# Holding only GpSimd's additions at a change of batch, in a kernel of four-way scans over an image

## The chip, the core and the metric

The kernel runs on one core of a Trainium2 chip. The metric is the device time of one execution in microseconds (us); of several executions the median is taken. A profile is one execution recorded by the hardware profiler; its times are counted from the start of its span.

## What is computed

The input `x` holds 4 images (the batch) of 128 channels and 96 by 96 pixels. Each image is normalised over groups of channels and laid out as four sequences of 9216 pixels: row by row (H), that reversed, column by column (V), and that reversed. Each sequence goes through the same block, the results are put back at their pixels, projected and added to `x`. Cut to what matters here:

```python
t = grouped1x1(x, in_proj_w, in_proj_b)            # 128 -> 512 channels
u, gate = t[:, :HID], t[:, HID:]
u = depthwise_conv(silu(u), dw_w)                  # 5 taps along the sequence
s = conv1x1(u, ssm_in_w); a = decay(conv1x1(u, ssm_delta_w))
bb = tanh(conv1x1(u, ssm_b_w)); cc = tanh(conv1x1(u, ssm_c_w))
prefix = cumsum(log(a))
hst = exp(prefix) * cumsum(bb * s * exp(-prefix))  # a linear recurrence
u = u + conv1x1(cc * hst + d * s, ssm_out_w)
y = conv1x1(grouped1x1(u * sigmoid(gate), mix_w), out_proj_w)
out = x + fuse_w @ concat(y of the four sequences) # with fuse_b
```

## The kernel before, in words

**Units and pairs.** Work is cut into units of 384 positions of one sequence. A unit has a batch, an order (V or H), a stage `st` of six, one of four interleaved phases `p`, and a direction `s` (0 forward, 1 reversed). The two directions of the same `st` and `p` make a pair; there are 384 units and 192 pairs, 48 to a batch: first 24 in V order, then 24 in H order. `pair(t)` issues everything of turn `t`. The order on every engine is written out by hand in the program (a manual schedule), and each engine takes its own instructions in that order.

**What one turn holds.** For pair `t` itself it computes the convolution of the first half of the channels on TensorE (`conv`, `conv_less`), the taps of the second half on VectorE (`taps`, L651), and the projections `proj`, 32 matmuls shown as `psum<-u,main`, with their Tanh and copies on ScalarE (L683, L684, L689) and the decay and drive on GpSimd (L691, L692). For pair `t+4` it computes the input projection and Silu (`front`, L495) where the sequence is fresh; the second half of each order reads the mirrored results of the first half back from DRAM. For the pair six turns back, `bi = 2*(t-6)`, it computes or rereads the gates (`gates_and_out`, Tanh at L537), multiplies by the state's output matrix (`out_of`, L520) and gates on VectorE (`gating`, L599 and L600). `recurrence` issues the scan on VectorE (L718) and the output steps on GpSimd (`outputs`, L724, L725 and the copy L727).

**The output products.** The gated units of turn `t` go to the list `waiting`. In the next turn `accumulate` multiplies each by the fused output matrix (16 matmuls, shown as `psum<-u,w_fin`), copies the result from PSUM to an SBUF tile `ys` on ScalarE (L751 with the bias, L753 without) and returns `add`, which adds `ys` to the accumulator `acc` on GpSimd (L770). `ys` has the pool's two buffers. `acc` is one tile for the whole image; it starts as the batch's `x` and ends as its output. A turn has two places for products: the first ahead of the gates (L845, bank `w[0]`) and the second either at L853, or behind the gating (L880, bank `w[1]`). Ahead of both come the turn's convolution matmuls.

**PSUM.** [...] The projections use banks 4 and 5 (`PROJ`). In a turn with a front, `plan` gives the convolution banks 4 and 5 and the products banks 7 and 6; in a turn without one, the convolution gets banks 7 and 6 and the products banks 4 and 5. The gates of a turn with a front go to banks 6, 4, 5 and 7.

**The change of batch.** When a batch's last additions are done, `send` issues four stores of `acc` on the DMA queue of SyncE (L733), and in the next turn four loads bring the next batch's `x` into the same places (L819), each behind its store. The first two units of the new batch come to their products in that turn. It is called `late`: `bi` is 98, 194 or 290, that is `t` = 55, 103 and 151. In a late turn the kernel before leaves the first place empty. It puts the first product in the second place and keeps its `add`; after the projections it issues that `add`, the whole second product (bank 6 again) and the second addition (L893 to L895):

```python
if waiting and not late:
    accumulate(waiting.pop(0), w[0], *final)()
...
if waiting:
    add = accumulate(waiting.pop(0), w[1])
    if not late:
        add()
...
proj(i, PROJ if back else banks, between)
...
if late:
    add()
    accumulate(waiting.pop(0), w[1])()
```

Turn 55 has a front, turn 56 has none. At the change from V to H inside a batch (turns 31 and 32 of the first) the same kinds of turn follow each other, and nothing is late there.

Of the kernel before, what the change touches and what calls it, by code (L numbers as in the profile page):

```python
# [42 lines left out]
F32 = mybir.dt.float32  # L43
# [4 lines left out]
P = 128  # L48
# [11 lines left out]
N = LN * WW // R  # L60
# [7 lines left out]
def conv_preact_kernel(  # L68
# [9 lines left out]
    nc = tc.nc  # L78
# [46 lines left out]
    def plan(with_front):  # L125

        return (PROJ, FRONT[:2]) if with_front else (FRONT[:2], PROJ)

    def bank(i):
        return psum[:, i, :]  # L130

    def mm(o, col, lhsT, rhs, start, stop):
        r = slice(32 * col, 32 * col + 32)
        nc.tensor.matmul(o[r, : rhs.shape[-1]], lhsT, rhs, start=start, stop=stop,  # L134
                         skip_group_check=True)
# [110 lines left out]
    def fresh(step):  # L246

        return step * UB < NU and step % NS < NS // 2
# [11 lines left out]
    def mirror(n):  # L260

        return None if n % NP < NP // 2 else NP - 1 - n % NP
# [124 lines left out]
    wk = ctx.enter_context(tc.tile_pool(name="work", bufs=2))  # L387
# [40 lines left out]
    def front(i, banks):  # L428
        for _ in front_parts(i, banks):
            pass  # L430
# [94 lines left out]
    def under(bi, s):  # L525

        seeded.add(bi)
        nc.scalar.copy(psum[:, SSM + 2 * s : SSM + 2 * s + 2, :N], us[bi][:, s])  # L528
# [21 lines left out]
    def load_kept(n):  # L550
        m = mirror(n)
        if n < NU // 2 - R and m is not None and m < NP // 2 - 2:
            old_gates[n] = gates[m % 2]
            nc.sync.dma_start(old_gates[n], kept[n // NP % 2][m])
# [58 lines left out]
    def conv(i, banks):  # L613

        step, p = units[i]["step"], units[i]["p"]
        sil, k, b0 = blocks(step), less_of(p), min(banks)
        for s in range(2):
            for g in range(4):
                mm(bank(b0 + s), g, band[:, s, p, g, :], columns(step, sil[s][:, g, :], 1 - k),
                   True, False)  # L620
# [15 lines left out]
    def new_u(i):  # L636
        us[i] = wk.tile([P, 2, 2, N], F32, tag="u", bufs=LAG + 2, name=f"u_{units[i]['id']}")
# [65 lines left out]
    def first_tap(i):  # L703
        if i < NU:
            taps(i, range(1))
# [25 lines left out]
    def send():  # L731
        for b, r in done:
            nc.sync.dma_start(out[b, :, r], accf[:, r])  # L733
            if b + 1 < B:
                reload.append((b + 1, r))
        done.clear()

    def accumulate(bu, bk, adder=nc.gpsimd, last=False):

        b, s, p, st = bu["b"], bu["s"], bu["p"], bu["st"]  # L740
        py = bank(bk)
        direct = last and (s == 1 or bu["order"] == "H")
        for j in range(2):
            for c in range(4):
                mm(py, c, w_fin[:, bu["dir"], j, 32 * c : 32 * c + 32], bu["v"][:, j, :],
                   j == 0, j == 1)
        y = py[:, :N]
        if not direct:
            ys = wk.tile([P, N], F32, tag="ys", name=f"ys_{bu['id']}")
            if s == 0 and bu["order"] == "H":  # L750
                nc.scalar.activation(ys, y, AF.Identity, bias=b_fin)  # L751
            else:
                nc.scalar.copy(ys, y)  # L753
            y = ys
        if s == 1:
            y, p, st = y[:, ::-1], R - 1 - p, NS - 1 - st
        if bu["order"] == "V":
            part = acc.rearrange("p (m q) r c -> p m q r c", q=R)[
                :, :, p, :, bass.ds(st * LN // R, LN // R)
            ]  # L760
            y = y.rearrange("p (c r m) -> p m r c", r=R, m=M)
        else:
            part = acc[:, bass.ts(st, LN), p, :]
            y = y.rearrange("p (h m) -> p h m", m=M)

        def add():
            if direct and s == 0:
                adder.scalar_tensor_tensor(part, y, b_fin, part, ALU.add, ALU.add)
            else:
                adder.tensor_add(part, y, part)  # L770
            if bu["order"] == "H" and bu["st"] >= NS // 2 and bu["p"] == R - 1:

                done.extend((b, bass.ts(2 * st + e, LN * WW // 2)) for e in range(2))

        return add
# [1 line left out]

    later, soon = [], []

    waiting = []  # L780

    def recurrence(t):
        i, k = 2 * t, t % R
        if k < 2 and 0 <= t // R - 1 < NU // UB:
            scan(t // R - 1, k)
        if 0 <= i - 10 < NU:
            outputs(i - 10)

    def head_banks(t):

        return PROJ if t % 2 or t >= LAG else FRONT[1::-1]

    def pair(t):
        i, k, bi = 2 * t, t % R, 2 * (t - LAG)
        back = bi >= 0
        old = back and mirror(bi // 2) is not None

        late = bi > 2 and (bi - 2) % (NU // B) == 0
        with_front = fresh((t + R) // R)
        final = (nc.vector, True) if t == NU // 2 - 1 else ()  # L800
        seed = old or back and not with_front

        ahead = old or back and not with_front
        banks, w = plan(with_front or not back)
        if not back:
            banks = head_banks(t)
        if back:
            front(t + R, FRONT)
        for n in soon:
            load_kept(n)  # L810
        soon.clear()
        if seed and not with_front:
            under(bi, 1)
        if t < NU // 2 - 2:
            send()

        if len(reload) == 4 and (k == 1 or late):
            for b, r in reload:
                nc.sync.dma_start(accf[:, r], xr[b, :, r])  # L819
            reload.clear()  # L820
        if t:
            new_u(i)
            taps(i, range(1, K))
            conv(i, banks)
        if t and not ahead:
            conv_less(i, banks)
        if not back:
            first_tap(i + 2)
            if t:
                front(t + R, FRONT if banks == PROJ else (5, 4, 2, 3))  # L830
        recurrence(t)
        un = units[i]
        stats_chunks(t)

        def stats_piece():
            if later and k > 1:
                next(later[0], None)

        if not ahead:
            free[0] = w[1]  # L840
            stats_piece()
        if seed and with_front:
            for s in (1, 0):
                under(bi, s)
        if waiting and not late:  # L845
            accumulate(waiting.pop(0), w[0], *final)()

        between = ahead and not old
        if between:
            conv_less(i, banks)  # L850
        if seed and not with_front:
            under(bi, 0)
        if ahead:  # L853
            accumulate(waiting.pop(0), w[1], *final)()
            free[0] = w[0]
            if not between:
                conv_less(i, banks)
            stats_piece()
        if old:
            scale_s(i - 2)  # L860
            for s in range(2):
                for j in range(2):
                    out_of(bi, s, j)
                load_gate(bi + s + UB)
        elif back:
            gates_and_out(bi, with_front)
        if back:
            for s in range(2):
                gating(bi, s)
        if un["order"] == "V" and un["b"] + 1 < B and un["st"] == NS - 1 and k == R - 1:  # L870
            later[:] = [stats_finish(un["b"] + 1)]
        if t + 1 < NU // 2:
            load_chunks(t + 1)
        if back:

            if k == 2 and t + 1 < NU // 2:
                soon.append(bi // 2 + 2)
            else:
                load_kept(bi // 2 + 2)
            if waiting:  # L880
                add = accumulate(waiting.pop(0), w[1])
                if not late:
                    add()
            first_tap(i + 2)
        if t == NU // 2 - 1:
            for s in range(2):
                under(bi + 2, s)
        if t == NU // 2 - 1:
            outputs(i - 8, None)
        proj(i, PROJ if back else banks, between)  # L890
        if not old and t > 0:
            scale_s(i - 2)
        if late:  # L893
            add()
            accumulate(waiting.pop(0), w[1])()  # L895
        if back:
            waiting.extend(units[bi : bi + 2])
        if t >= NU // 2 - 4:
            load_last(t)

        keep_silu((1, 2, 1, 0)[t] if t < R else 0)

        if bi > 0 and bi % (NU // B) == 0:
            send()
# [217 lines left out]
```

## Time and profile before

| what | value |
|---|---|
| median of 3 runs | 1839.7 us (1839.36 to 1840.79) |
| profiled execution, whole | 1833.3 us |
| its span, first to last instruction | 1831.6 us |
| TensorE, busy | 1806.8 us (99%) |
| ScalarE, busy | 1566.0 us (86%) |
| VectorE, busy | 1448.8 us (79%) |
| GpSimd, busy | 1423.5 us (78%) |
| granted TensorE clock, mean | 0.996 |

The lines of the profile that follow are read thus. PE is TensorE's matmuls, PEld its weight loads, DVE VectorE, ACT ScalarE, POOL GpSimd, SP SyncE; `L134` is line 134 of the kernel, and since all small matmuls go through one helper, their tiles tell them apart. In a table of waits, `PE psum L134 <- ACT ys L753: 3.1, 3, 1.1` says that TensorE stood still ahead of a matmul of L134 until ScalarE's L753 was done: 3.1 us in all, 3 times, 1.1 us at the longest. In a timeline a line has the start, the length, the engine, the line, the operation, output and inputs, and in brackets the idle time ahead of it. Matmuls overlap, and their ends are modelled.

### The profile page before, as it was taken

Reading aid. Unit: us, or ns where it says so; the run is one execution under the profiler, and the core shown is the slowest. Engines: PE = TensorE matmul, PEld = TensorE weight load, DVE = VectorE, ACT = ScalarE, POOL = GpSimd, SP = SyncE. Lnnn points to the kernel's source line nnn. Section 1 sums busy time; section 2 is a strip of 40 time slices with the busy share of each in tenths; the row PEclk is TensorE's granted clock in tenths of the full one; section 3 lists DMA queues with packets and bytes.
Section 4 is the critical chain, followed back from the end, with each engine's and each line's share of the span. In section 5 each row is a group of like instructions: output and inputs, shape, how many; then the busy total and the mean of one; then the engine's idle time right before and its main releaser. Section 6 shows DMA issues by size and latency. Waiting matters only on the chain.

```text
span 1831.6 us, 57282 instructions
## 1 busy us (share of the span) xinstructions
PE 1806.8 (99%) x24068; PEld 653.9 (36%) x24068; DVE 1448.8 (79%) x1451; ACT 1566.0 (86%) x2762; POOL 1423.5 (78%) x1469
## 2 busy tenths in 40 slices
PE   7999999999999999999999999999999999999998
PEld 4333333333333333333333333333333333333333
DVE  5888878877878888877778888877877778777886
ACT  4888888988888888888898888888888888888975
POOL 2487887778777888787877888787877788887785
PEclk8999999999999999999999999999999999999999
DMA  6755563444965566244696546443476634535434
GB/s 196 200 191 179 164 192 108 161 144 147 307 227 181 167 188 190 102 142 140 214 296 207 165 162 211 136 152 110 162 236 223 234 123 152 192 109 179 148 122 156
DMA packets 147825, 321.18 MB, mean 175 GB/s; under 512 B 14192, under 2 KB 115696, under 8 KB 147568
## 3 DMA queue, kind: packets, MB, share of 16 engines
q1 hardware_dynamic: 147136, 316.56, 53.1%
q8 instruction: 190, 3.11, 0.7%
q10 hardware_dynamic: 432, 0.96, 0.1%
q14 instruction: 67, 0.55, 0.1%
HBM read 185.21 MB, written 132.25 MB: 173 GB/s over the span
## 4 chain that ended last, share of the span: by engine, by line
PE 96%; ACT 2%; DMA 1%; DVE 1%; issue 0%; SPq 0%; POOL 0%; ACTq 0%; DVEq 0%; POOLq 0%
PE psum L134 82%; PE psum L520 8%; PE psum L514 5%; ACT sil L495 0%; DMA x_in<-in_xs 0%; DMA fuse<-in_fuse 0%; PE psum L286 0%; DVE u L600 0%; ACT t L701 0%; ACT t L689 0%; PE psum L364 0%; ACT psum L649 0%; DMA out<-acc 0%; ACT u L632 0%; DVE psum L651 0%
## 5 line engine op out<-in xcount | busy, mean ns | idle before, releaser
L651 DVE SCALAR_TENSOR_TENSOR psum<-sil,small,psum 128x768 f32<-128x768 f32 x576 | 588.9, 1022 | 33.2 <-ACT psum L649 7.4
L600 DVE SCALAR_TENSOR_TENSOR u<-gate,psum 128x768 f32<-128x768 f32 x376 | 349.6, 952 | 256.6 <-ACT gate L537 118.6
L134 PE MATMUL psum<-u,w_fin 128*32 128x384 f32 x6176 | 551.7, 487 | 0.2 <-ACT t L689 0.2
L134 PE MATMUL psum<-u,main 128*32 128x384 f32 x6144 | 536.4, 490 | 0.1
L770 POOL TENSOR_TENSOR acc<-ys,acc 128x384 f32<-128x384 f32 x374 | 412.2, 1122 | 33.3 <-ACT ys L751 9.1
L724 POOL TENSOR_TENSOR t<-t,t 64x384 f32<-64x384 f32 x191 | 234.9, 1230 | 158.4 <-PE psum L514 78.8
L134 PEld LDWEIGHTS psum<-u,w_fin 128*32 128x32 f32 x6176 | 189.1, 110 | 320.8 <-issue 218.7
L134 PEld LDWEIGHTS psum<-u,main 128*32 128x32 f32 x6144 | 181.6, 110 | 327.6 <-issue 199.1
L528 ACT COPY psum<-u 128x768 f32<-128x768 f32 x352 | 276.9, 800 | 20.7 <-DVE u L651 10.2
L691 POOL TENSOR_SCALAR t<-tm 64x384 f32<-64x384 f32 x191 | 177.0, 927 | 151.0 <-ACT tm L683 100.8
L134 PE MATMUL psum<-sil,band 128*32 128x384 f32 x3072 | 286.8, 489 | 3.1 <-ACT ys L753 3.1
L725 POOL TENSOR_TENSOR t<-t,t 64x384 f32<-64x384 f32 x191 | 246.4, 1290 | 15.0
L520 PE MATMUL psum<-t,main 32*128 32x384 f32 x1536 | 241.9, 513 | 3.3 <-ACT psum L528 2.6
L649 ACT ACTIVATE psum<-sil,small 128x768 f32<-128x768 f32 x192 | 174.1, 907 | 63.2 <-DVE u L600 53.7
L537 ACT ACTIVATE gate<-psum,bnorm 128x384 f32<-128x384 f32 x384 | 192.6, 582 | 28.9 <-PE psum L514 26.9
L692 POOL TENSOR_TENSOR t<-t,tm 64x384 f32<-64x384 f32 x192 | 195.0, 1016 | 15.4 <-ACT t L684 0.2
L651 DVE SCALAR_TENSOR_TENSOR u<-sil,small,psum 128x768 f32<-128x768 f32 x192 | 194.9, 1015 | 7.8
L495 ACT ACTIVATE sil<-psum,bnorm 128x385 f32<-128x385 f32 x384 | 191.7, 584 | 3.6 <-PE psum L134 1.4
L134 PE MATMUL psum<-sil,less 64*32 64x384 f32 x3072 | 168.2, 495 | 0.0
L514 PE MATMUL psum<-x_in,wn 32*128 32x384 f32 x768 | 162.0, 528 | 2.3 <-ACT u L632 1.2
L753 ACT COPY ys<-psum 128x384 f32<-128x384 f32 x281 | 129.9, 476 | 30.2 <-PE psum L134 29.2
L134 PEld LDWEIGHTS psum<-sil,band 128*32 128x32 f32 x3072 | 90.2, 109 | 175.6 <-issue 94.1
(92 smaller groups left out, 1500.3 us busy)
## 6 DMA issues: line engine op xcount, KB each, us to landing
sil<-sil SPq DMA_DIRECT2D x128, 770.0 KB, 6.7
kept<-gate SPq DMA_DIRECT2D x80, 768.0 KB, 3.7
gate<-kept SPq DMA_DIRECT2D x76, 768.0 KB, 5.2
x_in<-in_xs SPq DMA_DIRECT2D x192, 96.2 KB, 2.4
out<-acc SPq DMA_DIRECT2D x48, 384.0 KB, 8.0
acc<-in_xr SPq DMA_DIRECT2D x38, 384.0 KB, 6.9
xs<-in_xr SPq DMA_DIRECT2D x72, 192.0 KB, 4.7
x_in<-in_xs SPq DMA_DIRECT2D x184, 48.1 KB, 3.7
```

Of the source, the lines that this page charges most:

```text
L134: nc.tensor.matmul(o[r, : rhs.shape[-1]], lhsT, rhs, start=start, stop=stop, skip_group_check=True)
L495: nc.scalar.activation(sils[step][:, s, j, g, :], bank(bk)[:, : N + 1], AF.Silu, bias=bn[:, 1:2] if j else bn[:, 4 + g : 5 + g],)
L514: nc.tensor.matmul(bank(to)[:, :N], stats[un["b"]][0][r, s, :], x_in[s][r, q, off : off + N], start=True, stop=True)
L520: nc.tensor.matmul(bank(SSM + 2 * s + j)[:, :N], w_so[r, bass.ts(j, P)], z[r, :], start=bi not in seeded, stop=True, skip_group_check=True)
L528: nc.scalar.copy(psum[:, SSM + 2 * s : SSM + 2 * s + 2, :N], us[bi][:, s])
L537: nc.scalar.activation(gv[:, s, j, :], bank(to[2 * s + j])[:, :N], AF.Tanh, bias=bn[:, 2 + j : 3 + j], scale=0.5,)
L600: nc.vector.scalar_tensor_tensor(v, g, 1.0, pz, ALU.add, ALU.mult)
L651: nc.vector.scalar_tensor_tensor(us[i][:, :, 1, :] if k == K - 1 else part, src, w_tap[:, k : k + 1], part, ALU.mult, ALU.add,)
L692: nc.gpsimd.tensor_mul(ta[0:64, p, :], tb[0:64, :], tm[0:64, :])
L724: engine.tensor_mul(ta[0:64, p, :], tb[64:P, :], ta[64:P, p, :])
L725: engine.tensor_add(tb[0:64, :], ta[0:64, p, :], tb[0:64, :])
L770: adder.tensor_add(part, y, part)
```

## The change

At a late turn both products stay at the places that they have in every other turn. Only their two additions are kept, in a new list `held`, and issued in the next turn, behind that turn's `outputs` and ahead of its own first product. For that `ys` gets four buffers in place of two. The tile pools fill SBUF nearly to its end, so the program also reserves 512 bytes per partition for the dynamic DMA scratch in place of the default[...].

```diff
@@ accumulate
-            ys = wk.tile([P, N], F32, tag="ys", name=f"ys_{bu['id']}")
+            ys = wk.tile([P, N], F32, tag="ys", bufs=4, name=f"ys_{bu['id']}")
@@
-    waiting = []
+    waiting, held = [], []
@@ pair
-        if waiting and not late:
-            accumulate(waiting.pop(0), w[0], *final)()
+        for add in held:
+            add()
+        held.clear()
+        if waiting:
+            add = accumulate(waiting.pop(0), w[0], *final)
+            if late:
+                held.append(add)
+            else:
+                add()
@@
             if waiting:
                 add = accumulate(waiting.pop(0), w[1])
-                if not late:
+                if late:
+                    held.append(add)
+                else:
                     add()
@@
-        if late:
-            add()
-            accumulate(waiting.pop(0), w[1])()
@@ kernel
-    nc = bacc.Bacc("TRN2", target_bir_lowering=False, num_devices=1)
+    nc = bacc.Bacc(
+        "TRN2", target_bir_lowering=False, num_devices=1, dynamic_dma_scratch_size=512
+    )
```

## The prediction

> **What bounds the kernel now.** I read the page first: busy times, then the chain that ended last. TensorE is busy 99% of the span and carries 96% of that chain, at a granted clock of 0.996, so a microsecond counts only where TensorE's own stream is late.
>
> ```profile
> span 1831.6 us, 57282 instructions
> PE 1806.8 (99%) x24068; PEld 653.9 (36%) x24068; DVE 1448.8 (79%) x1451; ACT 1566.0 (86%) x2762; POOL 1423.5 (78%) x1469
> PE 96%; ACT 2%; DMA 1%; DVE 1%; issue 0%; SPq 0%; POOL 0%; ACTq 0%; DVEq 0%; POOLq 0%
> ```
>
> Second, the waits of TensorE (columns: total us, times, longest). All of them come to about 19 us; two rows belong to the changes of batch:
>
> ```profile
> PE psum L134 <- ACT ys L753: 3.1, 3, 1.1
> PE psum L514 <- ACT u L632: 1.2, 4, 0.4
> ```
>
> The first row's three waits are one at each change. Three of the second row's four, 0.28 us each, stand one pair earlier. Third, TensorE's timeline over the first change (start, length, operation). The two `u,main` rows here are the projections of pairs 55 and 56:
>
> ```profile
> 530.35 0.91 PE L514 MATMUL psum<-x_in,wn 32*128 32x384 f32 x2
> 531.54 0.96 PE L514 MATMUL psum<-x_in,wn 32*128 32x384 f32 x2 [0.28 <-ACT u L632]
> 533.41 1.50 PE L134 MATMUL psum<-u,w_fin 128*32 128x384 f32 x16
> 534.72 2.76 PE L134 MATMUL psum<-u,main 128*32 128x384 f32 x32
> 537.30 1.47 PE L134 MATMUL psum<-u,w_fin 128*32 128x384 f32 x16
> 539.83 1.50 PE L134 MATMUL psum<-sil,band 128*32 128x384 f32 x16 [1.05 <-ACT ys L753]
> 546.36 2.79 PE L134 MATMUL psum<-u,main 128*32 128x384 f32 x32
> ```
>
> In pair 55 the second gate matmul must wait until ScalarE has copied `u` (L632) out of its bank; the skipped first output product would have covered that wait. The second product (537.30) comes after the projection and fills bank 6, which the next pair's first convolution needs at once. The product ends at 538.77, but its copy stands on ScalarE behind the scaling at 538.65:
>
> ```profile
> 538.65 0.62 ACT L701 ACTIVATE t<-t,small 64x384 f32<-64x384 f32 x1
> 539.29 0.48 ACT L753 COPY ys<-psum 128x384 f32<-128x384 f32 x1
> ```
>
> Fourth, the length of pairs, from the start of one projection to the next (table of windows; first column after the window is its length, then each engine's busy us). The first two rows are pairs 31 and 32, where the scan order changes inside a batch and nothing is held; then pairs 55, 56 and 57:
>
> ```profile
> 302.39:312.63 10.24, 10.24 (x149) 3.82 (x144) 7.73 (x9) 9.00 (x18) 9.20 (x14) 1.00 0.28 101
> 312.63:321.71 9.08, 9.08 (x116) 3.36 (x108) 8.76 (x8) 7.46 (x13) 6.86 (x6) 1.00 0.54 185
> 524.55:534.72 10.17, 9.89 (x132) 3.63 (x128) 8.50 (x11) 8.43 (x16) 6.01 (x7) 1.00 0.94 316
> 534.72:546.36 11.64, 10.59 (x133) 3.79 (x125) 8.53 (x8) 7.86 (x14) 8.48 (x7) 1.00 0.73 260
> 546.36:555.47 9.11, 9.11 (x114) 3.39 (x113) 7.79 (x7) 8.16 (x15) 5.03 (x6) 1.00 0.60 196
> ```
>
> Both pairs of rows hold four output products. In order they take 10.24 + 9.08 = 19.32 us; at the change of batch 10.17 + 11.64 = 21.81 us. The other two changes have the same timelines to 0.05 us.
>
> [...] bank 6 is filled and wanted again with no group between. [...] the gaps show 0.28 + 1.05 = 1.33 us, the lengths 2.49. [...]
>
> **The change, part by part.** The built streams of both kernels differ in order only at the three changes (pairs 55, 103, 151); the number of instructions of each engine is the same.
>
> *Both products back at their places.* This is the order of pairs 31 and 32. Pair 55 gains a product (about 1.43 us from 308.22 to 309.64) ahead of the gates, which covers the `u` copy: in pair 54, which has both products, it costs 0.07 us over pair 55 (10.24 against 10.17). I checked what else that order asks of pair 55: `u`'s first bank is copied at about 531.4, and the gate that needs it would stand at about 532.2; the second product needs bank 6 emptied by the first gate's Tanh, as in pairs 31 and 54. Pair 55 becomes 10.24 (+0.07). Pair 56 loses the product after the projection and the wait behind it: 537.30 to 539.83, 2.53 us, and becomes 9.08 to 9.11. Sum: 21.81 − 19.32 or 19.35 = 2.46 to 2.49 us. With 2.47, three changes give 7.4 us.
>
> *Held additions.* They are held on GpSimd alone, and stand in pair 56 behind its output steps (L724 to L727) and ahead of the next two additions. Queued behind them are those two and L691/L692 of pair 56's decay. On my clock: projection 55 starts at 524.55 + 10.24 = 534.79, its Tanh (L683) ends 2.77 us later as after 524.55, L691 and L692 take 0.93 + 1.0 and end at 539.6, and the output steps take 1.2 + 1.2 + 0.5, one of them stretched to 2.55 as at 542.03 now. The held additions then start at about 544.2 and four of 1.2 us end at about 549.1. L691 and L692 follow to 551.2. The next L724 cannot start before the scan ends, 8.49 us after a projection (554.85 − 546.36), so at 543.9 + 8.49 = 552.4. GpSimd is 2.2 us later than now for one pair, and VectorE's scan hides all of it with 1.2 us over. Cost on the path: nothing. If that cover went, L727's copy has five more microseconds before the product that reads it (557.9 to 563.0).
>
> *The reload under them.* The additions need the new batch's x in `acc`. It landed at 539.32, 987.03 and 1431.70; now the second change's addition waits 1.22 us on it, but TensorE waits for none of that. Held, the additions start 2.5 to 6 us after the landing. SP's order is not moved.
>
> *Four copies.* A copy of unit 100's product (5.48 us after the projection, so at 549.4) needs unit 96's place, free at 545.4: 4.0 us in hand. With two copies unit 98's copy at 540.3 would wait 5.1 us, with ScalarE's queue behind it. Elsewhere ScalarE's `ys` copies now wait for GpSimd six times, 2.2 us in all; twin pairs without that wait are as long, so I take 0, bounds −2.2 and 0. That the semaphore of most copies goes is worth 17 ns each on ScalarE's sequencer, mostly behind waits for TensorE: 0.
>
> *Smaller scratch.* All tiles move down in SBUF by multiples of 512 bytes. No row shows what that costs; [...] so I take 0 and keep ±0.7 us, half the spread of the three runs (1.43).
>
> **The sum.** Against the profiled execution, 1833.3 us with a span of 1831.6: 1833.3 − 7.4 = 1825.9. That execution was 6.4 us under the median of the runs, with the same gaps; I take the same step off the median: 1839.7 − 7.4 = 1832.3.
>
> **The rivals.** *Only the visible gaps go.* If the pipelined rest comes back as slower matmuls or as a new wait of the second product for bank 6, 3 × 1.33 = 4.0 us is gained: 1835.7. For it: 1.15 us per change shows in no gap. Against it: pairs 31 and 32 do exactly this work in 19.32. *The wait moves on.* GpSimd's backlog reaches L727 or the fourth copy and the pair after pays what pair 56 gained: about 1839.7. Against it: margins of 1.2 and 4.0 us above. *Slower: the held additions wait for the reload.* Place: GpSimd in pair 56, then `ys` of unit 100 on ScalarE, then the output bank on TensorE. It decides from a landing about 7 us later than now (2.5 to 3.8 us to the addition, 4.0 to the copy); from there every microsecond is TensorE's. At 11 us late, three times 4 us are lost against 7.4 gained: 1844.3. For it: `acc` transfers here take up to 12.4 us to land. Against it: the chain that issues the reload stands ahead of all that changes, and its three landings spread over 2 us only. *That the change does nothing* is excluded by the built order.
>
> **How the numbers follow.** A measurement of this kernel tells about 0.2% (3.7 us) from no change. Forecast, 1832.3: 0.82. Visible gaps only, 1835.7, beside the line of 0.2%: 0.09. Wait moved on: 0.05. Slower: 0.04. Faster: the forecast and half of the second, 0.87; same 0.09; slower 0.04. The range runs from 1832.3 less 0.7 and about half of the 2.2 us of copies, 1830.4, up to the visible-gap case with its noise, 1836.0.
>
> **What would show it.** Right: TensorE's two rows of waits at the changes gone; pair 55 at 10.24 and pair 56 at 9.1; GpSimd with four L770 in a row in pair 56; L724 of pair 57 still waiting for the scan. Wrong: a gap at 532 or 533 (bank of `u` or bank 6), ScalarE's `ys` waiting for GpSimd in pair 57, a pair 57 over 9.11, or a change of length far from the three changes, which would be the addresses.

## The result and the profile after

| | before | after |
|---|---|---|
| median of 6 executions each | 1837.27 us (1835.08 to 1840.79) | 1827.03 us (1824.34 to 1830.29) |
| after over before | | 0.9948, 95% interval 0.9932 to 0.9964 |
| profiled execution | 1833.3 us, span 1831.6 | 1830.29 us, span 1828.6 |
| granted clock of that execution, mean | 0.996 | 0.993 |

The kernel became faster by 0.52% (0.36% to 0.68%), where 7.4 us or 0.40% were forecast; the two medians alone lie 10.2 us apart. The time itself, 1827.03 us, lies below the range that the prediction gave (1830.4 to 1836.0).

The page after, busy times and chain. TensorE still carries 96% of the chain, as before.

```profile
span 1828.6 us, 56926 instructions
PE 1805.3 (99%) x24068; PEld 653.1 (36%) x24068; DVE 1451.0 (79%) x1451; ACT 1566.5 (86%) x2762; POOL 1423.7 (78%) x1469
PE 96%; ACT 1%; DVE 1%; DMA 1%; issue 0%; SPq 0%; DVEq 0%
```

TensorE's waits after (total us, times, longest). The row of L134 for `ys` is gone, and of the four waits of L514 for `u` (L632) one is left. The wait for `mv` (L187) is new in this execution; it stands at 20.25 us, in the start, and is taken up below.

```profile
PE psum L187 <- DVE mv L184: 2.1, 1, 2.1
PE psum L514 <- ACT u L632: 0.4, 1, 0.4
```

TensorE's timeline over the first change. A product (535.08) now stands ahead of the gates of pair 55 and another (538.13) ahead of its projections (539.45). Behind the projections there is no product and no gap: the convolution of pair 56 (542.03) follows at once.

```profile
535.08 1.50 PE L134 MATMUL psum<-u,w_fin 128*32 128x384 f32 x16
536.50 0.73 PE L514 MATMUL psum<-x_in,wn 32*128 32x384 f32 x3
538.13 1.50 PE L134 MATMUL psum<-u,w_fin 128*32 128x384 f32 x16
539.45 2.76 PE L134 MATMUL psum<-u,main 128*32 128x384 f32 x32
542.03 1.47 PE L134 MATMUL psum<-sil,band 128*32 128x384 f32 x16
548.55 2.79 PE L134 MATMUL psum<-u,main 128*32 128x384 f32 x32
```

The table of windows after, for pairs 55, 56 and 57. Pair 56 went from 11.64 to 9.10 us. Pair 55 kept its length to 0.01 us, though it now holds one product more, and pair 57 kept its own.

```profile
529.27:539.45 10.18, 10.18 (x148) 3.80 (x144) 8.57 (x11) 8.88 (x18) 6.09 (x7) 1.00 0.93 313
539.45:548.55 9.10, 9.10 (x116) 3.37 (x108) 8.78 (x8) 7.41 (x13) 5.95 (x5) 1.00 0.92 329
548.55:557.66 9.11, 9.11 (x113) 3.39 (x112) 8.32 (x8) 8.15 (x15) 7.17 (x8) 1.00 0.62 204
```

GpSimd in pair 56, where the held additions lie: four of L770 in a row, the two held ones and the turn's own two, behind the output steps (L727) and ahead of the decay (L691). L691 starts 5.26 us after the projection at 548.55; before it was 2.99 us (549.35 less 546.36). `L724` of pair 57 still waits 1.69 us for VectorE's scan (L718), so GpSimd's backlog has been absorbed before it reaches anyone.

```profile
547.04 1.85 POOL L727 COPY t<-t 64x384 f32<-64x384 f32 x1
548.97 4.76 POOL L770 TENSOR_TENSOR acc<-ys,acc 128x384 f32<-128x384 f32 x4
553.81 0.92 POOL L691 TENSOR_SCALAR t<-tm 64x384 f32<-64x384 f32 x1
557.51 1.24 POOL L724 TENSOR_TENSOR t<-t,t 64x384 f32<-64x384 f32 x1 [1.69 <-DVE t L718]
```

**Where the time went.** The two profiled spans differ by only 3.0 us (1831.6 to 1828.6), less than half of the forecast gain. To see why, I cut each execution into three by fixed instructions: up to the projection of pair 6, from there to the projection of pair 191, and the end. In each row of the table of windows the first number after the window is its length; the third from the end is the granted clock. First the kernel before:

```profile
0.00:79.05 79.05, 68.27 (x893) 30.51 (x893) 50.18 (x83) 53.79 (x110) 26.57 (x54) 0.94 0.67 198
79.05:1792.95 1713.90, 1706.96 (x22843) 611.11 (x22841) 1375.66 (x1338) 1494.11 (x2625) 1378.66 (x1399) 1.00 0.54 175
1792.95:1831.58 38.63, 31.55 (x340) 12.33 (x336) 22.93 (x30) 18.12 (x29) 18.23 (x18) 0.96 0.45 164
```

Then the kernel after:

```profile
0.00:83.89 83.89, 70.67 (x892) 30.84 (x892) 50.25 (x83) 53.95 (x110) 25.92 (x53) 0.88 0.64 187
83.89:1789.93 1706.04, 1703.04 (x22842) 609.82 (x22840) 1377.75 (x1338) 1494.55 (x2625) 1379.58 (x1400) 1.00 0.54 175
1789.93:1828.57 38.64, 31.55 (x340) 12.49 (x336) 22.97 (x30) 18.03 (x29) 18.18 (x18) 0.92 0.46 164
```

The 185 pairs in the middle, which hold all three changes of batch and run at full clock, are 7.86 us shorter. The start is 4.84 us longer: there TensorE was granted half its clock for 20.5 us in this execution (20.4 to 34.1 and 40.9 to 47.7), against 10.2 us before (16.1 to 19.5 and 36.6 to 43.4). The code of the start is the same in both. Here the row for `mv` comes in: in the execution after, the first eight matmuls that fill the start (L286, at 14.51) ran at full clock and took 3.68 us, TensorE stood still for 2.1 us, and the half clock followed; in the execution before, with half clock from 16.1, the same eight (at 15.86) took 5.38 us and lasted until L187. −7.86 + 4.84, with 0.01 at the end, is the −3.0. Pair by pair, the 7.86 is made of pairs 56, 104 and 152 (11.63 to 9.10 or 9.11 each, 7.57 in all), and of seven pairs with one product ahead of the gates and one behind them (31, 54, 79, 102, 127, 150, 175), each 10.24 before and 10.18 after, 0.4 in all; pair 76 is 0.1 longer.

### The profile page after: what moved, and what is told of

Read it like the earlier page. It is cut to its first block, busy times and chain, and to the rows that moved or that the text cites. A ratio compares the mean times of both kernels' runs of the same rounds, so it can differ in the third digit from the quotient of the medians.

```text
span 1828.6 us, 56926 instructions
## 1 busy us (share of the span) xinstructions
PE 1805.3 (99%) x24068; PEld 653.1 (36%) x24068; DVE 1451.0 (79%) x1451; ACT 1566.5 (86%) x2762; POOL 1423.7 (78%) x1469
## 4 chain that ended last, share of the span: by engine, by line
PE 96%; ACT 1%; DVE 1%; DMA 1%; issue 0%; SPq 0%; DVEq 0%
PE psum L134 83%; PE psum L520 8%; PE psum L514 5%; DMA acc<-in_xr 0%; DVE bn L282 0%; ACT sil L495 0%; DVE u L600 0%; ACT psum L649 0%; DMA x_in<-in_xs 0%; DVE psum L651 0%; PE psum L286 0%; ACT psum L528 0%; PE psum L199 0%; ACT u L632 0%; ACT t L689 0%
## 5 line engine op out<-in xcount | busy, mean ns | idle before, releaser
L134 PE MATMUL psum<-u,w_fin 128*32 128x384 f32 x6176 | 552.3, 487 | 0.2 <-ACT t L689 0.2
L134 PE MATMUL psum<-u,main 128*32 128x384 f32 x6144 | 536.4, 490 | 0.2
L770 POOL TENSOR_TENSOR acc<-ys,acc 128x384 f32<-128x384 f32 x374 | 410.7, 1119 | 31.2 <-ACT ys L751 9.2
L724 POOL TENSOR_TENSOR t<-t,t 64x384 f32<-64x384 f32 x191 | 232.2, 1216 | 154.6 <-DVE t L718 70.8
L134 PEld LDWEIGHTS psum<-u,w_fin 128*32 128x32 f32 x6176 | 188.8, 110 | 321.7 <-issue 216.5
L134 PEld LDWEIGHTS psum<-u,main 128*32 128x32 f32 x6144 | 182.0, 110 | 328.1 <-issue 198.9
L691 POOL TENSOR_SCALAR t<-tm 64x384 f32<-64x384 f32 x191 | 177.1, 927 | 153.7 <-ACT tm L683 100.1
L134 PE MATMUL psum<-sil,band 128*32 128x384 f32 x3072 | 287.2, 491 | 0.0
L692 POOL TENSOR_TENSOR t<-t,tm 64x384 f32<-64x384 f32 x192 | 195.1, 1016 | 15.4 <-ACT t L684 0.2
L134 PE MATMUL psum<-sil,less 64*32 64x384 f32 x3072 | 168.1, 495 | 0.0
L514 PE MATMUL psum<-x_in,wn 32*128 32x384 f32 x768 | 157.5, 527 | 1.5 <-DVE bnorm L239 1.1
L727 POOL COPY t<-t 64x384 f32<-64x384 f32 x188 | 141.0, 750 | 15.5 <-PE psum L134 3.6
L134 PEld LDWEIGHTS psum<-sil,band 128*32 128x32 f32 x3072 | 90.8, 109 | 171.8 <-issue 95.5
```

Of the source, the lines that this page charges most:

```text
L514: nc.tensor.matmul(bank(to)[:, :N], stats[un["b"]][0][r, s, :], x_in[s][r, q, off : off + N], start=True, stop=True)
L692: nc.gpsimd.tensor_mul(ta[0:64, p, :], tb[0:64, :], tm[0:64, :])
L724: engine.tensor_mul(ta[0:64, p, :], tb[64:P, :], ta[64:P, p, :])
```

## The experiments

All use the same input and the metric of the first section. "Middle" is the stretch from the projection of pair 6 to that of pair 191, 1713.90 us before and 1706.04 after. The theory was the prediction's: 7.4 us come from the products' order at the three changes, the held additions are hidden, and the buffers serve only to make that legal.

### Buffers and scratch alone

```diff
-            ys = wk.tile([P, N], F32, tag="ys", name=f"ys_{bu['id']}")
+            ys = wk.tile([P, N], F32, tag="ys", bufs=4, name=f"ys_{bu['id']}")
...
-    nc = bacc.Bacc("TRN2", target_bir_lowering=False, num_devices=1)
+    nc = bacc.Bacc(
+        "TRN2", target_bir_lowering=False, num_devices=1, dynamic_dma_scratch_size=512
+    )
```

This is the kernel before with these lines and nothing else.

> The kernel before with four copies of ys and the small scratch alone; both products and additions of the late turns stay as they were. My theory (the gain of the change sits in the late turn and the one after it, and what was measured beyond it is the clock at the start): pairs 55 and 56 stay at 10.17 and 11.63, the time is that of before within 0.1% (ratio 0.999 to 1.001). Rival (the buffers or the addresses bring a part everywhere): ratio 0.998 to 0.9985, some 3 us, with pairs shorter far from the changes of batch. The seven pairs at 10.24 in before and 10.18 in the changed kernel tell which edit that small step belongs to: 10.18 here if it is the buffers or the waits that go with them.

Measured: ratio to before 1.0003 (0.9990 to 1.0017), middle 1713.58 us. The pairs at the changes stayed as before (pair 56 at 11.63), and the seven pairs came to 10.18. Buffers and scratch are worth 0.3 us, as the theory had it: 0.4 less in the seven pairs, 0.1 more in pair 76.

### Only the first product back at its place

The kernel after, with the second product of a late turn behind the projections again; both additions stay held.

```diff
-            if waiting:
-                add = accumulate(waiting.pop(0), w[1])
-                if late:
-                    held.append(add)
-                else:
-                    add()
+            if waiting and not late:
+                accumulate(waiting.pop(0), w[1])()
...
+        if late:
+            held.append(accumulate(waiting.pop(0), w[1]))
```

> The changed kernel with only the first product of a late turn back at its place; the second is made after the projections again, in bank 6, and both additions are held. My theory has two separate stalls of about equal size: pair 55 holds one product and no wait for the copy of u, so 10.24 less 1.31 = 8.9 us; pair 56 keeps the product and the wait behind it, 11.6 us. Both together 20.5, a gain of 1.25 per change, half of the whole. Rival (one cause, the wait for bank 6): pair 55 stays near 10.2 and the gain is 0.

Measured: ratio 0.9989 (0.9974 to 1.0004), middle 1711.67, pairs 55 and 56 at 9.28 and 11.88, each 0.3 to 0.4 us over what was expected. The time alone doesn't tell this kernel from before; the lengths of the pairs do. TensorE's timeline of this kernel at the first change:

```profile
542.62 2.79 PE L134 MATMUL psum<-u,main 128*32 128x384 f32 x32 [0.35 <-ACT gate L537]
547.96 1.50 PE L134 MATMUL psum<-sil,band 128*32 128x384 f32 x16 [1.27 <-ACT ys L753]
```

The wait for `u` is covered, but with nothing ahead of them the projections now wait 0.35 us for the gate's Tanh to leave their bank, and the wait for `ys` behind them is still there, 1.27 us. The gain is 0.64 us of 2.53 per change (21.80 to 21.16), where the theory had 1.25 and the rival nothing. So the larger part of the gain comes only with the second product at its place, and the product ahead of the projections covers a wait of its own that the prediction had not listed.

### Additions at once

The kernel after, with both products at their places and their additions issued in the same turn, as in every other turn.

```diff
-            if late:
-                held.append(add)
-            else:
-                add()
+            add()
```

(The same four lines go at the second product.)

> The changed kernel with nothing held: the two additions of a late turn are issued at once and stand on GpSimd ahead of L691 and L692 of that turn. They wait for the reload (about 5 us after the projection of pair 55). Theory: GpSimd stands for 6 to 7 us, L692 of pair 55 ends at about +9 in place of +4.8 after its projection, the scan of pair 56 waits for it 2 to 3 us, and TensorE shows 0 to 2 us per change in pair 56 or 57; total between the changed kernel and 6 us above it. Rival (the additions need not be held at all): pair lengths as in the changed kernel, 10.2, 9.1, 9.1.

Measured: ratio 1.0009 (0.9998 to 1.0019), middle 1714.49. Pair 56 is 9.10 or 9.11 us as in the kernel after, but the pairs behind it, 57, 105 and 153, take 11.78, 13.75 and 10.32 instead of 9.11: 8.5 us lost where 7.6 were gained. At most 6 were expected, and 0 to 2 at a change; the measured losses are 2.7, 4.6 and 1.2. GpSimd at the first change (the releaser printed in the brackets ended early; the addition starts as the new batch's `x` lands in `acc`):

```profile
540.84 2.39 POOL L770 TENSOR_TENSOR acc<-ys,acc 128x384 f32<-128x384 f32 x2 [7.34 <-ACT psum L528]
543.32 0.88 POOL L691 TENSOR_SCALAR t<-tm 64x384 f32<-64x384 f32 x1
544.28 1.01 POOL L692 TENSOR_TENSOR t<-t,tm 64x384 f32<-64x384 f32 x1
```

The chain to TensorE then runs over VectorE, which waits with its scan for L692, ScalarE, which waits for VectorE's gating, and the next product on TensorE. One line from each of their timelines:

```profile
545.33 2.87 DVE L718 TENSOR_TENSOR_SCAN t<-t,t 64x768 f32<-64x768 f32 x1 [2.77 <-POOL t L692]
```

```profile
549.22 0.91 ACT L649 ACTIVATE psum<-sil,small 128x768 f32<-128x768 f32 x1 [3.18 <-DVE u L600]
```

```profile
550.67 1.50 PE L134 MATMUL psum<-u,w_fin 128*32 128x384 f32 x16 [1.90 <-ACT tm L683]
```

The trace shows what stands behind the waiting additions: GpSimd waited 7.34 us, then did 2.39 us of additions, and L691 and L692, which do not need the reload, started only then, at 543.32 and 544.28. ScalarE's Tanh that L691 reads (L683) had ended at 538.35, 5.0 us earlier. Holding the additions moves that wait away from them. This is near the prediction's slower rival ("the held additions wait for the reload"): without the hold the wait on GpSimd is real and costs 1.2 to 4.6 us per change. But it reaches TensorE over the decay and the scan, not over `ys` and the output bank as that rival had it.

### The old order at four more places

The kernel before, with the same late order also at the four changes from V to H inside a batch (turns 31, 79, 127 and 175). Nothing is reloaded there.

```diff
+        apart = bi > 2 and (bi - 2) % (NU // B // 2) == 0
...
-        if waiting and not late:
+        if waiting and not apart:
...
-                if not late:
+                if not apart:
...
-        if late:
+        if apart:
```

> The kernel before with its late order also at the four changes from V to H inside the batches, seven places in place of three. Theory (a price per place): pairs 31 and 32 of the first batch and their likes in the others go from 10.24 and 9.09 to about 10.17 and 11.6, 2.5 us each, 9.9 us in all, ratio 1.0054. Rival (the price hangs on the reload and the transfers of the change of batch): at these places nothing is stored or loaded in between, so less than 1 us each, ratio under 1.002.

Measured: ratio 1.0053 (1.0033 to 1.0073), middle 1724.36, that is +10.5 us; pairs 32, 80, 128 and 176 went from 9.08 or 9.09 to 11.91, 11.63, 11.63 and 11.63. The same two waits appeared at each new place (first one here):

```profile
315.57 0.96 PE L514 MATMUL psum<-x_in,wn 32*128 32x384 f32 x2 [0.25 <-ACT u L632]
323.86 1.50 PE L134 MATMUL psum<-sil,band 128*32 128x384 f32 x16 [1.05 <-ACT ys L753]
```

So the order alone costs 2.5 to 2.8 us a time, without any reload near it, and the rival (under 1 us) is out. The prediction read the price from pairs 31 and 32; this puts it back there and finds it.

### Two copies of `ys`, and three

The kernel after with `bufs=2`, once, and with `bufs=3` and the default scratch.

```diff
-            ys = wk.tile([P, N], F32, tag="ys", bufs=4, name=f"ys_{bu['id']}")
+            ys = wk.tile([P, N], F32, tag="ys", bufs=2, name=f"ys_{bu['id']}")
```

> The changed kernel with two copies of ys in place of four. Theory: in pair 56 the copy of the next product needs the place of a held one, which is free only some 5 us later; ScalarE stands, and TensorE behind it; pair 56 becomes 12 to 15 us in place of 9.1, so the gain of 7.9 is lost and the time is 0 to 8 us above before. Rival (the four copies are not needed): pairs 55 and 56 as in the changed kernel.

Measured, one execution: middle 1724.84 us, 18.8 more than after; pairs 56, 104 and 152 at 14.61, 14.62 and 14.58. ScalarE's copy of unit 98 waits 5.45 us for GpSimd's addition (5.1 were forecast), and TensorE 3.7 us for ScalarE at the longest. The middle is 10.9 us over that of the kernel before, where 0 to 8 were expected: pairs 57, 105 and 153, in which half clock follows, are 0.5 to 0.8 us longer besides, 2.0 in all, which the expectation didn't count.

```profile
550.02 0.48 ACT L753 COPY ys<-psum 128x384 f32<-128x384 f32 x1 [5.45 <-POOL acc L770]
```

```profile
PE psum L514 <- ACT ys L753: 10.9, 3, 3.7
```

```diff
-            ys = wk.tile([P, N], F32, tag="ys", bufs=4, name=f"ys_{bu['id']}")
+            ys = wk.tile([P, N], F32, tag="ys", bufs=3, name=f"ys_{bu['id']}")
...
-    nc = bacc.Bacc(
-        "TRN2", target_bir_lowering=False, num_devices=1, dynamic_dma_scratch_size=512
-    )
+    nc = bacc.Bacc("TRN2", target_bir_lowering=False, num_devices=1)
```

> The changed kernel with three copies of ys and the default scratch (there is room for the third). Theory: the first product of pair 56 has a place, its second must wait for the first held addition, about 3 us; pair 56 or 57 is longer by 0 to 2.5 us, and the gain is between 2 and 8 us. It also tells the small step of the seven pairs apart: 10.18 again if it comes with more copies, 10.24 if it came with the scratch's size. Rival (three do as well as four): pair lengths as in the changed kernel.

Measured with three: ratio 1.0032 (1.0018 to 1.0045), middle 1714.85, pairs 56, 104 and 152 at 12.11, 12.05 and 12.05. These are 2.9 to 3.0 us over the kernel after, where 0 to 2.5 were expected, and the gain of 2 to 8 us that was to be left isn't there.

```profile
545.48 0.48 ACT L753 COPY ys<-psum 128x384 f32<-128x384 f32 x1 [2.93 <-POOL acc L770]
```

The wait of ScalarE falls from 5.45 through 2.93 to none with two, three and four copies. Four is the least that keeps the gain: held additions keep two tiles over a turn in which two more are filled. Three copies are even slower than the kernel before: the middle is 1.0 us longer in the profile, and 16 of the 20 executions had a clock of 0.992 or less. Half clock after the three stalls (6.5 us in all), as with two copies, may be the reason in some executions, but this is an estimate: the profiled one (0.995) shows none in the middle, so it isn't shown. The seven pairs are 10.18 with three copies and the default scratch, and 10.24 with two copies and the small one: the 0.06 us go with the copies, not with the scratch.

### The level: repeats, and a warmed start

The difference was now explained to a few tenths, but the time was 5.3 us under the forecast. What was open was the level: whether the kernel before has stretches at half clock in the middle that the change avoids, or whether only the start differs. First the kernel after once more and the kernel before once, no edit in either.

> The changed kernel once more, for a second profile and more runs. Theory (the change is worth what the pairs show, some 8 us, and the level of a run is set by TensorE's clock in the first 70 us): the stretch from the projection of pair 6 to that of pair 191 is 1706.0 us again within 0.3, the start differs by up to 10 us between profiles, and the ratio to before is 0.9945 to 0.9965. Rival (the change gives something besides, which the pairs of one profile do not show): ratio under 0.9945 with the stretch again 1706.

> The kernel before once more, for a second profile. Theory: pairs 55 and 56 again 10.17 and 11.63 at all three changes, the stretch from pair 6 to pair 191 again 1713.9 within 0.3; the start differs. Rival (the price of the change of batch in the kernel before hangs on when the reload lands, as in the kernel without holding): pair 56 or 57 longer at one change or another, by up to 2 us.

Measured: after again 1826.66 us, ratio 0.9942 (0.9922 to 0.9962), middle 1706.07, start 78.69. The middle is as the theory had it; the ratio lies just on the rival's side of 0.9945, and its interval covers both, so the time doesn't decide. Before again 1834.44 in its one execution, middle 1713.86, start 79.05, with pair 56 and its likes at 11.63 at all three changes. The middle of each kernel repeats to 0.04 us; the start of the kernel after doesn't (83.89 and 78.69).

Then two more single executions of the kernel before.

> The kernel before again, for one more profile of it. Theory A: wherever its clock comes out, every half-clock window lies in the first 70 us or the last 25, and the stretch from pair 6 to pair 191 is 1713.9 us. Theory B: if this execution has a mean clock of 0.992 or less, a half-clock window stands at a change of batch (about 545, 990 or 1437 us) and the stretch is longer by 1.5 us or more for each.

> As the one before it: one more profile of the kernel before. Theory A: half-clock windows only in the first 70 us and the last 25, stretch 1713.9 us. Theory B: with a mean clock of 0.992 or less, one at a change of batch and a longer stretch.

Measured: 1839.93 us and 1835.31 us, middles 1713.96 and 1714.00. The first is the slowest profiled execution of this kernel, and its start is a long one, as in the first profile of the kernel after. Its table of windows, up to 34.2 us:

```profile
0.00:34.20 34.20, 25.90 (x228) 15.92 (x236) 15.29 (x46) 14.39 (x35) 9.49 (x36) 0.80 0.67 219
```

and the same of the kernel after:

```profile
0.00:34.20 34.20, 25.64 (x220) 15.73 (x220) 15.16 (x46) 14.21 (x35) 9.49 (x36) 0.80 0.66 217
```

The clock is 0.80 in both (0.95 in this stretch of the first profile of before), this execution too has the 2.1 us wait for `mv`, and pair 6 is reached at 84.67 and 83.89. Taken against this execution, the span after is 9.6 us shorter (1838.2 to 1828.6): 7.9 in the middle, 0.9 at the end and 0.8 at the start. None of the four profiles of the kernel before has a stretch at half clock in the middle, not even this one with a clock of 0.992. So theory B is not seen; the 12 executions at 0.991 or less (of the 92 in the table further down) were not profiled.

Last, both kernels with a fuller start: six filling matmuls instead of four, and three more in the first pair, where TensorE waits for `x_in`.

```diff
-    for _ in range(4):
+    for _ in range(6):
         stay_busy(512)
...
             if i == 0 and (e, j) == (0, 1):
+                for _ in range(3):
+                    stay_busy(512, 3)
                 front(R, (5, 4, 2, 3))
```

> The kernel before with more filling matmuls at its start: six in place of four ahead of the first statistics product, and three in the wait of the first projection for x_in (results unused). Theory A (the runs of one kernel differ by the clock of the first 70 us alone): the half-clock windows of the start go, the spread of 12 us shrinks to 3 or less, the time is 3 to 6 us under the median of before, ratio 0.997 to 0.998. Theory B (the stalls at the changes of batch also cost half-clock windows in some executions of the kernel before): the spread stays 5 us or more, with clocks of 0.993 to 0.995 beside 0.998.

> The same filling in the changed kernel, which has no stall at the changes of batch. Theory A: 7.9 us under the kernel before with the filling, and the same small spread. Theory B: the spread shrinks here and not there, and the distance is 9 to 11 us. Both: under the changed kernel by 2 to 5 us, so some 1822 to 1824 us.

Measured: before with it 1835.98, ratio 0.9991 (0.9975 to 1.0006); after with it 1825.76, ratio 0.9937 (0.9916 to 0.9958), not to be told from after itself (0.9948, 0.9942). Both miss the times that were expected (ratio 0.997 to 0.998, and 1822 to 1824 us), and the hoped-for narrow spread did not come: 14 executions of the first spread over 8.5 us, and in the profiled one the wait for `x_in` had only moved, to 63.8 us, with half clock from 62.3 to 69.1. One of its pairs 56 took 12.03 us, since the reload landed late and `ys` waited 0.35 us for GpSimd: the kernel before isn't free of that risk either. The difference between the two medians is 10.2 us. By their signs these are theory B's outcomes (a spread of 5 us or more, a distance of 9 to 11). But the kernel after with the same filling, which has no such stall, spread over 7.2 us in 8 executions, and the profiled middle of the kernel before with it (1714.61 us) holds no half clock. So neither theory is settled. No version beats the kernel after by more than the measurement can tell.

## Why the prediction was right and wrong

**The change of order: right.** Both rows of waits went at the changes, pair 56 came to 9.10 (9.08 to 9.11 forecast), the three changes gave 2.52 or 2.53 us each where 2.46 to 2.49 were forecast. The rival that only the visible gaps go is out: 1.33 us per change show as gaps and 2.5 were gained, and the experiment on V to H gave the same 2.5 back.

**The length of pair 55: a little off.** Forecast 10.24, measured 10.18. This is the step on the four copies, which took 0 for them, with bounds of −2.2 and 0: with three or four copies each of the seven such pairs is 0.06 us shorter, −0.4 in all. The six waits of `ys` for GpSimd that the prediction counted don't explain it, since only two of them lie in these seven pairs (31 and 127). Where the 0.06 us come from isn't shown.

**The held additions: right.** They start 9.5 us after projection 55 (9.4 forecast), end 14.3 after it (14.3), L691 is 2.3 us late (2.2), and L724 still waits for the scan, with 1.69 us over (1.2). They hold nothing up. The rival "the wait moves on" would show in pair 57, which is still 9.11; two and three copies show, in pair 56, what it would have looked like.

**The reload: right.** It landed at 545.0, 989.48 and 1431.15, 3.6 to 6.0 us ahead of the held additions (2.5 to 6 forecast). Without the hold the wait for it costs what the change brings.

**The smaller scratch: right.** No cost within what the runs can tell (1.0003, 0.9990 to 1.0017, together with the copies). The forecast's 0 for the scratch was the author's estimate.

**The sum: wrong, and this is the step that failed.** It took 7.4 us off the median of three executions, 1839.7, and read the 6.4 us between that median and the profiled execution as a fixed step that could be carried over. It isn't fixed. It is the level of the executions at hand, which in the profiles goes with how long the start (and the end) runs at half clock: in the first profile of before the clock was 0.94 up to pair 6 at 79.05, in the slowest one 0.88 up to 84.67. Three more executions of the same kernel gave 1835.16, 1835.08 and 1835.18, so that the median of six is 1837.27. In all, 92 executions of the kernel before whose clock is listed lie between 1831.6 and 1846.5 us, and sort by that clock (the rows that both kernels have):

| mean granted clock | executions of before | their mean, us | executions of after | their mean, us |
|---|---|---|---|---|
| 0.991 | 10 | 1843.6 | 1 | 1835.6 |
| 0.993 | 3 | 1840.3 | 1 | 1830.3 |
| 0.995 | 16 | 1836.9 | 5 | 1827.7 |
| 0.996 | 22 | 1835.5 | 1 | 1825.7 |
| 0.997 | 5 | 1832.5 | 4 | 1824.9 |

The median that the forecast started from lies where the executions at 0.992 lie (25 of before, mean 1840.5; the clocks of those three executions are not listed). The page's own execution, with 0.996, was no outlier but another draw. Against 1837.27 the same 7.4 gives 1829.9, which misses by 2.8 instead of 5.3; 0.5 of these 2.8 is the middle (7.86 gained, not 7.4), and the rest lies outside it. The sum's other line, 1825.9 off the profiled execution, came within 1.1 us of the measured median, but in part by luck, since that execution was such a draw. The range was too narrow for the same reason: it held bounds for scratch and copies, and nothing for the level, though three executions and a profile of one kernel already lay 7.5 us apart (1833.3 to 1840.79).

**What stays open.** At equal clock, weighting the rows by the executions of after, the gain is 8.7 us (three of the five rows have a single execution of after). The middle shows 7.9. The end shows about 0.9 more in some comparisons: it takes 38.6 us when it holds one stretch of 3.4 us at half clock ahead of its last matmul, as in the three profiles of the kernel after (one of them with the fuller start) and in one of before, and 39.6 to 39.8 when it holds 6.8, as in the other three of before. The ratios say 9.6 and 10.7 us, with intervals that reach down to 6.6 and 7.0. The rest of it goes with which clocks were drawn: 10 of 12 executions of after were at 0.995 or more, and 45 of 92 of before. Whether that is chance, or whether the shorter middle changes the end, the runs don't settle.

## What to carry to other kernels

Find the same pair of stages where nothing is held, and price a disturbed order by the whole length of it and not by the gaps that show: here 2.5 us against 1.33. Where a wait must stay, put it on the instruction that needs it and let that stand behind everything else that its engine has to do (with the additions at once, L691 started 5.0 us after its input was there), with a buffer for each result that waits meanwhile (four here; three lost the gain and more). And forecast a difference, not a time: cut both executions at fixed instructions, keep start and end apart from the steady middle, and give a time its level from many executions, with the spread of that level in the range.

## What the runs showed of the hardware

The steady middle of 185 pairs repeats to 0.14 us in 1714 over four profiles of the kernel before, while the whole time of one unchanged kernel spread over 15 us in 92 executions. In the profiled executions start and end account for the differences: pair 6 was reached at 77.8 to 87.9 us over the profiles here, with a mean granted clock of 0.98 and 0.86 up to it.

In the kernels before and after, the granted clock of the profiled executions was 1.00 or 0.50. The stretches at 0.50 that end inside the span are 3.4 and 6.8 us long in the kernel before, and 3.4, 6.8 and 13.7 us in the kernel after. In each of three traces they begin whole multiples of 3.413 us apart: in the kernel before at 16.11, 36.59 and 1811.52 (6 and 520 such steps), in the kernel after at 20.42, 40.90 and 1809.00 (6 and 518), and with two copies at 551.62, 1002.18 and 1452.74, which is 132 steps each time.

What TensorE did ahead of them differs. With two copies these three stretches follow TensorE's stalls of about 3.6 us (10.9 in all). In the kernel after, TensorE stood still 2.1 us at the start and was busy for 1.35 of the 3.41 us ahead of 20.42, and the next 13.7 us were at half clock. In the kernel before, half clock from 16.11 us follows 3.41 us (12.70 to 16.11) in which the profile has TensorE busy throughout, most of it with matmuls of a single column (L379).

Nor does the size of a hole alone tell these cases apart; what does isn't shown. In the kernel with buffers alone the wait at the start was 2.4 us, and no half clock followed it: the mean clock up to pair 6 (77.77) was 0.98, against 0.88 in the kernel after. With the additions at once the stall of pair 105, 2.8 us, was followed by a stretch at 998.6, and those of pairs 57 (1.90 us) and 153 by none. The twelve stalls of 1 us in the four profiles of the kernel before were followed by none.
